# Conditional layer on quarters of TensorE, last contexts one product later, first block's weight sums one by one

## The chip, the cores and the metric

The kernel runs on one core of a Trainium2 chip. The metric is the device time of one execution in microseconds (us), the median of several runs. The profiler recorded one execution more; its times, and its "span" from the first to the last instruction, are what the views below show. The engines are TensorE (PE, with its weight loads as PEld), VectorE (DVE), ScalarE (ACT), GpSimd (POOL) and SyncE (SP), which here only issues DMAs. [...]

## What is computed

`x` is 64 batches of 64 rows with 1024 columns, 4096 tokens in all. Everything is float32, except where the last part quantises. Cut to what matters:

```python
def cond(x, condition, weights):            # weights: 16 x 64 x 64
    W = weights[condition]                  # one 64 x 64 matrix for each batch
    return einsum('bct,bcd->bdt', x, W)

def attn(x, qkvw, qkvb, ow, ob):            # 32 heads of 32
    q, k, v = split(x @ qkvw + qkvb)
    probs = softmax(q @ k.T / sqrt(32))     # within a batch of 64 rows
    return (probs @ v) @ ow + ob

x = x + attn(cond(x, itok, cond_weights), ...)
x = x + ffn(cond2(x, ...), ...)             # routed low-rank layer, quantised gated layer
```

Only the conditional layer, the attention and the first part of its output projection are touched by the change. The rest (`second_stage`) follows and stays as it is.

## The kernel before

**Tiling.** Two batches make a tile of 128 partitions (`x_t`), four tiles a block of 512 tokens (`PB = 4`), and there are `NBLK = 8` blocks. All large products (queries, keys, values, output) use a Winograd form of Strassen's scheme: a matrix of weights is cut in quarters A11 to A22 and a matrix of tokens in quarters B11 to B22, and seven products of quarters replace eight. Four sums of weight quarters (S1 to S4) and four of token quarters (T1 to T4) are needed. The products are issued in `Winograd.ORDER = (1, 6, 7, 5, 2, 4, 3)`; the weights are A11, S2, S3, S1, A12, A22, S4 and the tokens B11, T2, T3, T1, B21, T4, B22. Products 1 and 2 share a PSUM bank, as do 7 and 4, and 5 and 3: what was in the bank must have been read before the second one adds to it. In the profile the products appear by bank: `psqa`, `psqb`, `psqc`, `psqd`, then a, c and d again; `psk..` for keys, `psv..` for values, `po..` for the output. A query or key product is 8 matmul instructions in the trace, a value product 16: each matmul of float32 shows as two passes.

**The conditional layer.** `conditional(b, tiles)` makes B11 to B22 of a block. For each tile `j` of 128 tokens (two batches), the two 64x64 weights are gathered by POOL into `wg` and copied beside the diagonal's zeros into a 128x128 tile `wbd[j]` (L323, L375). A matmul (L350) then has 128 columns of `x` as the loaded operand and `wbd[j]` as the streaming one. Eight steps per block (`hf` for the half of the columns, `j` for the tile) have four matmuls each, in a bank of `ps_g`, which has four buffers. VectorE (L356, even `j`) or ScalarE (L358, odd `j`) copies the bank to `B`, and VectorE makes T1 to T4 (L366, L371) as soon as their quarters are there.

**The hand-written order.** `run(cost, product, rest)` issues PE's product, then the `rest` (copies, sums) of the product before (the list `behind`), and adds `cost` to a planned time `now`. Before each product it issues everything in `due` whose planned time has come. `phase(b, c, fills, length)` sets two groups of attention per phase (`group`, at the start and at half of the length): scores (L491, on quarters of TensorE, 64x64), the softmax on VectorE and ScalarE, a parting into halves of words (`ph`), a DMA transpose (`phT`), a joining (`pT`, ScalarE), and, in a later group, the context (L543). There are four phases per block. In the last one the `fills` between are the conditional layer, the first values job and the first query and key jobs of the block that follows. In the very last phase the fills are 14 products of the output projection, and the last contexts are set by `at(now + 41, contexts)`.

**Block 0.** The weights are loaded raw and S1 to S4 are made on the way: by VectorE for the first query job, by POOL for the first key and values jobs (`first_sums`), later by VectorE. `load_qk` and `load_v_raw` hand back a function that issues all four sums and the store; it is issued in one piece behind a product (`product_and_sums`, `with_sums`). In later blocks the sums are loaded from DRAM.

Of the kernel before, what the change touches and what calls it, by code (L numbers as in the profile page):

```python
# [182 lines left out]
def attention(tc, a, x_t, ctx_d, ident, dram, ps_g, KC, PB, NBLK, NCH, HPC, H, C, chores, early, op):  # L183
# [27 lines left out]
    with ExitStack() as ctx, ExitStack() as mid:  # L211
# [54 lines left out]

        RAW = ("A11", "A21", "A22", "A12")

        def sums(eng, at):
            eng.tensor_tensor(at("S1"), at("A21"), at("A22"), ALU.add)  # L270
            eng.tensor_tensor(at("S2"), at("S1"), at("A11"), ALU.subtract)
            eng.tensor_tensor(at("S3"), at("A11"), at("A21"), ALU.subtract)
            eng.tensor_tensor(at("S4"), at("A12"), at("S2"), ALU.subtract)

        w_qk, w_v = {}, {}
        later = []
# [1 line left out]
        def load_qk(b, wh, c, eng=None):  # L278
            t = w_qk[b, wh, c] = wp.tile([P, 7, KQ, P], F32, tag="wqk", name=f"w{wh}_{b}_{c}")
            if b == 0:  # L280
                if (wh, c) == ("q", 0):
                    held(t[:, SLOT["A11"], 0, 0:1], x_next[0][1])
                for key in RAW:
                    nc.sync.dma_start(t[:, SLOT[key], :, :], quarter(key, (0 if wh == "q" else H) + c * P, P))
                def rest():
                    sums(eng or nc.vector, lambda key: t[:, SLOT[key], :, :])
                    nc.gpsimd.dma_start(qk_d[wh, c], t)
                return rest
            nc.sync.dma_start(t, qk_d[wh, c])

        def load_v(b, g, slot):
# [3 lines left out]
        def load_v_raw(g, eng):  # L295
            for slot in range(7):
                w_v[0, g, slot] = w.tile([P, KQ, VC], F32, tag=f"wv{slot}", name=f"wv{slot}_0_{g}")

            def at(key):
                return w_v[0, g, SLOT[key]]  # L300

            for key in RAW:
                nc.sync.dma_start(at(key), quarter(key, 2 * H + g * VC, VC))

            def rest():
                sums(eng, at)
                for slot in range(7):
                    later.append(lambda slot=slot: nc.gpsimd.dma_start(v_d[g][:, slot, :, :], w_v[0, g, slot]))
            return rest

        bqkv = act.tile([P, 3 * KC], F32, tag="bqkv", name="bqkv")
        x_next = load_x(0)
        first_sums = [load_qk(0, "q", 0), load_qk(0, "k", 0, nc.gpsimd)]
        nc.sync.dma_start(bqkv, a["qkvb_t"])
        first_sums.append(load_v_raw(0, nc.gpsimd))

        wbd = []  # L320
        for j in range(PB):
            t = w.tile([P, P], F32, tag=f"wbd{j}", name=f"wbd{j}")
            nc.vector.memset(t, 0.0)  # L323
            wbd.append(t)
        kbd, vbd = [], []
        for u in range(4):
            t = act.tile([P, 2, HB], F32, tag=f"kbd{u}", name=f"kbd{u}")
# [8 lines left out]

        def conditional(b, tiles):

            def one(hf, j):
                key = f"B{hf + 1}{j // 2 + 1}"  # L340
                box = []

                def product():
                    xt = tiles[j][0]
                    if j % 2 == 0:
                        B[key] = yp.tile([P, KQ, HB], F32, tag=key, name=f"y{key}_{b}")
                    ps = ps_g.tile([P, 4, P], F32, tag="g", name=f"cond_{b}_{j}_{hf}")
                    for q in range(KQ):
                        k = hf * KQ + q
                        nc.tensor.matmul(ps[:, q, :], xt[:, k * P:(k + 1) * P], wbd[j], start=True, stop=True)  # L350
                    box.append(ps)

                def rest():
                    dst = B[key][:, :, (j % 2) * P:(j % 2 + 1) * P]
                    if j % 2 == 0:
                        nc.vector.tensor_copy(dst, box[0])  # L356
                    else:
                        nc.scalar.copy(dst, box[0])  # L358
                    if (hf, j) == (0, 3):
                        t_of("T1", "B12", "B11")  # L360
                    elif (hf, j) == (1, 3):
                        t_of("T2", "B22", "T1")
                        t_of("T3", "B22", "B12")
                    elif (hf, j) == (1, 1):
                        B["T4"] = B["B12"]
                        nc.vector.tensor_tensor(B["T4"], B["B21"], B["T2"], ALU.subtract)  # L366
                return 0.95, product, rest

            def t_of(key, x, y):
                B[key] = yp.tile([P, KQ, HB], F32, tag=key, name=f"{key}_{b}")  # L370
                nc.vector.tensor_tensor(B[key], B[x], B[y], ALU.subtract)  # L371

            for j, (_, wg) in enumerate(tiles):
                for r in range(2):
                    (nc.gpsimd if b else nc.vector).tensor_copy(wbd[j][halves[r], halves[r]], wg[halves[r], :])  # L375
            return [one(0, j) for j in range(PB)] + [one(1, j) for j in (2, 3, 0, 1)]

        def job(name, cost, n, matmuls, put, begin=None, done=None):


            banks, u = {}, {}

            def one(i):
                def product():
                    if i == ORDER[0] and begin:
                        begin()
                    bank = BANK[i]
                    first = bank not in banks
                    if first:
                        banks[bank] = ps_g.tile([P, 512], F32, tag="g", name=name.format(bank))  # L390
                    matmuls(i, banks[bank], first)
                    if done:
                        done(i)

                def rest():
                    ps = banks[BANK[i]][:, 0:n]
                    if i == 1:
                        u[1] = p1.tile([P, 512], F32, tag="p1", name=name.format("p1"))[:, 0:n]
                        nc.scalar.copy(u[1], ps)
                    elif i in (6, 7):  # L400
                        u[i] = p1.tile([P, 512], F32, tag=f"u{i}", name=name.format(f"u{i}"))[:, 0:n]
                        nc.vector.tensor_tensor(u[i], ps, u[1 if i == 6 else 6], ALU.add)
                    else:
                        m, t, v = {5: (1, 1, 7), 2: (0, 0, None), 4: (1, 0, 6), 3: (0, 1, 6)}[i]
                        put(m, t, ps, u.get(v))
                return cost, product, rest

            return [one(i) for i in ORDER]

        def biased(dst, ps, bias, u):  # L410
            if u is None:
# [1 line left out]
            else:  # L413
                nc.vector.scalar_tensor_tensor(dst, ps, bias, u, ALU.add, ALU.add)  # L414

        def rows_job(b, c, wh, next_load):

            qT = None

# [24 lines left out]
                if i == ORDER[-1] and next_load:  # L444
                    next_load()

            return job(f"ps{wh}{{}}_{b}_{c}", 1.72, HB, matmuls, put, begin, done)

        def values_job(b, g, next_load):

# [170 lines left out]
        def qk_fill(b, c):  # L621
            fills = []
            for wh in "qk":
                n = qk_jobs.index((b, wh, c))

                def next_load(n=n):
                    if n + 2 < len(qk_jobs):
                        f = load_qk(*qk_jobs[n + 2])
                        if f:
                            pending_sums.append(f)  # L630

                js = rows_job(b, c, wh, next_load)
                if b == 0 and n >= 2:

                    cost, product, rest = js[5]

                    def product_and_sums(product=product):
                        product()
                        if pending_sums:
                            pending_sums.pop(0)()  # L640
                    js[5] = (cost, product_and_sums, rest)
                fills += js
            return fills

        v_raw = []

        def v_fill(b, g):
            def next_load(slot):
                if b == 0 and g + 1 < NV:
                    if slot == SLOT[A_OF[ORDER[-1]]]:  # L650
                        v_raw.append(load_v_raw(g + 1, nc.vector))
                    return
                nxt = (b, g + 1) if g + 1 < NV else (b + 1, 0)
                if nxt[0] < NBLK:
                    load_v(*nxt, slot)
            js = values_job(b, g, next_load)
            if (b, g) == (0, 0):
                cost, product, rest = js[4]

                def product_and_sums():  # L660
                    product()
                    pending_sums.pop(0)()
                js[4] = (cost, product_and_sums, rest)
            return js

        for f in conditional(0, x_next):
# [7 lines left out]
        for b in range(NBLK):  # L674
            if b + 1 < NBLK:
                x_next = load_x(b + 1)
            for c in range(NP):
                fills, length = [], None
                if c + 1 < NP:
                    fills += qk_fill(b, c + 1)  # L680
                    if c == 0:
                        fills[7:7] = v_fill(b, 1)
                        if b == 0:
                            cost, product, rest = fills[4]

                            def with_sums(product=product):
                                product()
                                v_raw.pop()()
                            fills[4] = (cost, with_sums, rest)
                elif b + 1 < NBLK:  # L690

                    fills += conditional(b + 1, x_next) + v_fill(b + 1, 0) + qk_fill(b + 1, 0)
                else:
# [2 lines left out]
                    op.open_rest()  # L696
                    fills += op.pair(0) + op.pair(1)
                    length = 24
                    at(now + 41, contexts)
                if b + 1 == NBLK and c == 1:  # L700
                    assert next(chores, None) is None
                    early.close()
# [972 lines left out]
```

## Time and profile before

| | us |
|---|---|
| three runs | 2479.37, 2483.23, 2483.56 (median 2483.23) |
| the profiled execution | 2482.55 |
| its span, first to last instruction | 2480.8 |
| PE busy | 2435.7 (98% of the span) |
| DVE busy | 1524.9 (61%) |
| ACT busy | 953.6 (38%) |
| POOL busy | 360.8 (15%) |
| mean granted clock of TensorE | 0.992 of full |

The chain that ended last is "followed back from the last instruction: at each step to what released it, or to the instruction before it on its engine":

```profile
PE 95%; DVE 3%; DMA 1%; issue 1%; ACT 0%; SPq 0%; ACTq 0%; DVEq 0%
```

All waits of PE for another engine that last more than 3 us in total (us in total, times, longest):

```profile
PE cond L350 <- DVE wbd L375: 9.2, 1, 9.2
PE qTp_u L1427 <- DVE qb_u L1420: 7.2, 1, 7.2
PE c L543 <- ACT pT L533: 5.9, 1, 5.9
PE qTp_i L1427 <- DVE qb_i L1420: 3.9, 2, 2.8
PE cond L350 <- DVE yB L356: 3.2, 7, 0.5
```

The first is the start of the kernel, the second and fourth lie in its last 40 us, which the change doesn't touch. How to read a line of the views: in the chain, start, duration, engine, what, source line and number of merged instructions; in the utilisation of a stretch, its bounds and length, then the busy time of PE, PEld, DVE, ACT and POOL with the number of instructions, the granted clock, the busy share of the DMA engines and GB/s. "issue" is time in which an engine waited for nothing that the profile shows.

### The profile page before, as it was taken

What the parts mean: (1) busy time and instruction counts of PE and PEld (TensorE: products, weight loads), DVE (VectorE), ACT (ScalarE), POOL (GpSimd) and SP (SyncE); (2) the same over time, 40 slices, a digit from 0 to 9 for tenths busy, and PEclk for the clock granted to TensorE, in tenths of its full rate; (3) what the DMA queues carried; (4) which work ended last, traced back from release to release, by engine and by line L of the source; (5) the groups of instructions that cost most, each with busy time, mean ns of one, the idle gap of its engine ahead of it and who ended that gap; (6) DMA issues with size and microseconds to landing.
All of it is one profiled execution on the core that took longest, in us unless ns stands there. A gap on an engine that the chain in (4) does not pass through costs nothing.

```text
span 2480.8 us, 34182 instructions
## 1 busy us (share of the span) xinstructions
PE 2435.7 (98%) x13232; PEld 1703.8 (69%) x13232; DVE 1524.9 (61%) x2957; ACT 953.6 (38%) x1303; POOL 360.8 (15%) x451
## 2 busy tenths in 40 slices
PE   8999999999999999999999999999999999999996
PEld 7888888888888888888888644444454545454452
DVE  4585585675764755745646623333367777778787
ACT  1243353443443533533534533343423333333333
POOL 5010011011122221110000233334200000000001
PEclk9999999999999999999999999999999999999997
DMA  8795767676677667766646668877744443434343
GB/s 281 262 266 153 225 192 232 191 208 203 205 201 246 206 188 248 201 202 181 171 145 215 187 213 248 271 232 239 227 151 79 87 79 81 85 73 91 71 96 70
DMA packets 417980, 446.76 MB, mean 180 GB/s; under 512 B 299665, under 2 KB 353938, under 8 KB 404114
## 3 DMA queue, kind: packets, MB, share of 16 engines
q1 hardware_dynamic: 387298, 377.90, 52.5%
q0 software_dynamic: 12080, 49.82, 7.6%
q10 hardware_dynamic: 18432, 16.79, 2.0%
q8 instruction: 106, 1.74, 0.3%
q14 instruction: 64, 0.52, 0.1%
HBM read 272.97 MB, written 100.66 MB: 151 GB/s over the span
## 4 chain that ended last, share of the span: by engine, by line
PE 95%; DVE 3%; DMA 1%; issue 1%; ACT 0%; SPq 0%; ACTq 0%; DVEq 0%
PE pska L428 5%; PE psva L455 5%; PE poc L1019 5%; PE pskc L428 4%; PE psvc L455 4%; PE pskd L428 4%; PE psqd L428 4%; PE pbc L1019 4%; PE pba L1019 4%; PE psvd L455 4%; PE psqa L428 4%; PE poa L1019 4%; PE pod L1019 4%; PE pbd L1019 4%; PE psqc L428 4%; PE s L491 3%
## 5 line engine op out<-in xcount | busy, mean ns | idle before, releaser
L533 ACT COPY pT<-phT 128x1024 int16<-128x1024 int16 x128 | 167.2, 1342 | 84.8 <-DMA phT<-ph 84.6
L553 ACT ACTIVATE co<-c,bqkv 128x256 f32<-128x256 f32 x128 | 60.6, 473 | 295.2 <-PE c L543 253.6
L503 DVE TENSOR_REDUCE mx<-s 128x8 f32<-128x512 f32 x128 | 88.3, 690 | 138.0 <-PE s L491 128.4
L521 ACT COPY ph<-prob 128x1024 int16<-128x1024 int16 x128 | 131.4, 1046 | 43.4 <-DVE prob L515 42.7
L414 DVE SCALAR_TENSOR_TENSOR kbd<-pskd,bqkv,psku 32x256 f32<-32x256 f32 x256 | 122.6, 479 | 30.9 <-PE pskd L428 27.2
L507 ACT ACTIVATE prob<-prob 128x512 f32<-128x512 f32 x128 | 78.9, 628 | 154.4 <-DVE prob L504 130.6
L1140 POOL TENSOR_TENSOR xo<-xo,ob 128x1024 f32<-128x1024 f32 x32 | 82.5, 2597 | 375.7 <-DMA xo<-in_x_dram 371.2
L428 PE MATMUL psqa<-yB,wq 128*128 128x256 f32 x512 | 123.5, 384 | 0.0
L428 PE MATMUL pska<-yB,wk 128*128 128x256 f32 x512 | 122.6, 382 | 0.0
L1483 POOL DMA_DIRECT2D out_dram<-y x29 | 25.2, 869 | 653.4 <-DVE y L1475 653.4
L1114 ACT COPY xh<-xo 128x1024 int16<-128x1024 int16 x64 | 64.1, 1040 | 143.8 <-DVE xo L1159 143.4
L455 PE MATMUL psva<-wv,yB 128*128 128x256 f32 x512 | 117.7, 383 | 0.0
L1019 PE MATMUL poa<-woA,cx 128*128 128x512 f32 x256 | 115.3, 593 | 0.0
L1019 PE MATMUL pba<-wtA,x1T 128*128 128x512 f32 x256 | 115.1, 592 | 0.0
L1125 ACT COPY xTo<-xhT 128x1024 int16<-128x1024 int16 x64 | 84.8, 1341 | 64.1 <-DMA xhT<-xh 62.3
L455 PEld LDWEIGHTS psva<-wv,yB 128*128 128x128 f32 x512 | 96.8, 191 | 13.4
L428 PEld LDWEIGHTS pska<-yB,wk 128*128 128x128 f32 x512 | 96.0, 190 | 14.3 <-issue 1.4
L428 PEld LDWEIGHTS psqa<-yB,wq 128*128 128x128 f32 x512 | 95.2, 190 | 13.7 <-issue 0.2
L513 DVE TENSOR_REDUCE den<-prob 128x8 f32<-128x512 f32 x128 | 86.8, 678 | 17.4 <-ACT prob L507 17.2
L504 DVE TENSOR_TENSOR prob<-s,mx 128x512 f32<-128x512 f32 x128 | 88.6, 692 | 9.7 <-DVE mx L503 0.9
L515 DVE TENSOR_TENSOR prob<-prob,den 128x512 f32<-128x512 f32 x128 | 89.8, 702 | 4.4
L412 ACT ACTIVATE kbd<-pska,bqkv 32x256 f32<-32x256 f32 x128 | 59.6, 466 | 79.2 <-PE pska L428 77.6
(243 smaller groups left out, 5138.5 us busy)
## 6 DMA issues: line engine op xcount, KB each, us to landing
wv<-v_d SPq DMA_DIRECT2D x98, 512.0 KB, 3.8
wq<-q_d SPq DMA_DIRECT2D x28, 1792.0 KB, 8.1
wk<-k_d SPq DMA_DIRECT2D x28, 1792.0 KB, 8.2
x<-in_x_dram SPq DMA_DIRECT2D x32, 512.0 KB, 9.8
ctx_d<-co ACTq DMA_DIRECT2D x128, 128.0 KB, 5.6
cx<-ctx_d SPq DMA_DIRECT2D x16, 1024.0 KB, 7.0
xo<-in_x_dram SPq DMA_DIRECT2D x32, 512.0 KB, 5.7
xT_d<-xTo SPq DMA_DIRECT2D x64, 256.0 KB, 4.1
```

The source lines that it names most:

```text
L414: nc.vector.scalar_tensor_tensor(dst, ps, bias, u, ALU.add, ALU.add)
L428: nc.tensor.matmul(ps[:, 0:HB], A[:, SLOT[A_OF[i]], k, :], B[B_OF[i]][:, k, :], start=first and k == 0, stop=k == KQ - 1, skip_group_check ...
L455: nc.tensor.matmul(ps[:, j * VC:(j + 1) * VC], B[B_OF[i]][:, k, j * P:(j + 1) * P], A[:, k, :], start=first and j == 0 and k == 0, stop=k ...
L503: nc.vector.tensor_reduce(mx_v, ps, AX.X, ALU.max)
L504: nc.vector.tensor_tensor(p.rearrange("p (a e) k -> p a e k", a=2), ps, mx_v.unsqueeze(3).to_broadcast([P, 2, HPC, C]), ALU.subtract)
L513: nc.vector.tensor_reduce(den, p, AX.X, ALU.add)
L515: nc.vector.tensor_tensor(p, p, den.unsqueeze(2).to_broadcast([P, n, C]), ALU.mult)
L521: nc.scalar.copy(h, planes(p.rearrange("p n k -> p (n k)")))
L533: nc.scalar.copy(planes(pT.rearrange("p a b q -> p (a b q)")), hT)
L1019: self.nc.tensor.matmul(ps, self.B[self.B_OF[i]][:, k, :], self.A[self.A_OF[i]][:, k, :], start=first and k == 0, stop=k == self.KQ - 1, s ...
L1125: nc.scalar.copy(planes(xT.rearrange("p k q -> p (k q)")), hT)
L1140: nc.gpsimd.tensor_add(s["x"][:, t, :], s["x"][:, t, :], self.ob)
```

## The change

Four things are changed.

1. The conditional layer works on 64x64 quarters of TensorE. There is no `wbd`; the gathered `wg` streams directly. Each of four steps per block makes a whole tile `j`, with two banks (one for each half of the rows, that is for each batch) and 32 matmuls of 64x64x64. VectorE empties the first bank and ScalarE the second, each in two copies of 256 columns. T1 to T4 all come after the last tile. The planned costs are four times 1.2 in place of eight times 0.95.
2. Sums of weights are a list of four instructions instead of one function. They are issued one or two at a time ahead of products (`with_sums`): the `wv` sums one each ahead of fills 3 to 6, the query and key sums two each ahead of products 5 and 6 of a job.
3. The very first query job takes its products in the order (1, 2, 6, 7, 5, 4, 3). As 1 and 2 share a bank, the rest of 1 is issued ahead of 2.
4. The last contexts are planned at 44.5 instead of 41, which is one product of the output projection later.

```diff
-        def sums(eng, at):
-            eng.tensor_tensor(at("S1"), at("A21"), at("A22"), ALU.add)
...
+        def sums(eng, at, stored):
+            def last():
+                eng.tensor_tensor(at("S4"), at("A12"), at("S2"), ALU.subtract)
+                stored()
+            return [
+                lambda: eng.tensor_tensor(at("S1"), at("A21"), at("A22"), ALU.add),
+                lambda: eng.tensor_tensor(at("S2"), at("S1"), at("A11"), ALU.subtract),
+                lambda: eng.tensor_tensor(at("S3"), at("A11"), at("A21"), ALU.subtract),
+                last,
+            ]
...
-            def one(hf, j):
+            def one(j):
+                banks = []
                 def product():
-                    for q in range(KQ):
-                        k = hf * KQ + q
-                        nc.tensor.matmul(ps[:, q, :], xt[:, k * P:(k + 1) * P], wbd[j], start=True, stop=True)
+                    xt, wg = tiles[j]
+                    for r in range(2):
+                        banks.append(ps_g.tile([P, KC, C], F32, tag="g", name=f"cond{r}_{b}_{j}"))
+                    for k in range(KC):
+                        for r, f in ((0, 0), (1, 1), (0, 1), (1, 0)):
+                            nc.tensor.matmul(
+                                banks[r][halves[f], k, :], xt[halves[r], k * P + f * C:k * P + (f + 1) * C],
+                                wg[halves[r], :], start=True, stop=True,
+                            )
                 def rest():
+                    for hf in range(2):
+                        key = f"B{hf + 1}{j // 2 + 1}"
+                        if j % 2 == 0:
+                            B[key] = yp.tile([P, KQ, HB], F32, tag=key, name=f"y{key}_{b}")
+                        for r in range(2):
+                            t0 = (j % 2) * P + r * C
+                            src = banks[r][:, hf * KQ:(hf + 1) * KQ, :]
+                            if r == 0:
+                                nc.vector.tensor_copy(B[key][:, :, t0:t0 + C], src)
+                            else:
+                                nc.scalar.copy(B[key][:, :, t0:t0 + C], src)
+                    if j == PB - 1:
                         t_of("T1", "B12", "B11")
                         t_of("T2", "B22", "T1")
                         t_of("T3", "B22", "B12")
                         B["T4"] = B["B12"]
                         nc.vector.tensor_tensor(B["T4"], B["B21"], B["T2"], ALU.subtract)
-                return 0.95, product, rest
+                return 1.2, product, rest
-            return [one(0, j) for j in range(PB)] + [one(1, j) for j in (2, 3, 0, 1)]
+            return [one(j) for j in range(PB)]
...
+                    if order[1] == i == 2:
+                        behind.pop()()
...
-                js = rows_job(b, c, wh, next_load)
+                js = rows_job(b, c, wh, next_load, (1, 2, 6, 7, 5, 4, 3) if n == 0 else ORDER)
                 if b == 0 and n >= 2:
-                    js[5] = (cost, product_and_sums, rest)
+                    for at_, count in ((5, 2), (6, 2)):
+                        with_sums(js, at_, pending_sums, count)
...
+        def with_sums(fills, i, sums, count):
+            cost, product, rest = fills[i]
+            def product_and_sums():
+                for _ in range(min(count, len(sums))):
+                    sums.pop(0)()
+                product()
+            fills[i] = (cost, product_and_sums, rest)
...
                         if b == 0:
-                            fills[4] = (cost, with_sums, rest)
+                            for at_ in range(3, 7):
+                                with_sums(fills, at_, v_raw, 1)
...
-                    at(now + 41, contexts)
+                    at(now + 44.5, contexts)
```

## The prediction

> **What bounds the kernel now.** I read the page first: PE is busy 98% of 2480.8 us and has 95% of the chain of waits. A change can only pay where that chain leaves PE, or where it makes PE's own stream shorter. So I then read the chain in order of time around the three places that the diff touches, and single instructions on the timeline. First a block boundary (0 to 1; the other six have the same starts to 0.1 us):
>
> ```profile
> 181.62 1.08 PE s L491 x32
> 182.72 0.70 DVE mx L503
> 183.52 0.69 DVE prob L504
> 184.21 0.38 DVE kbd L414
> 186.11 0.69 DVE yB L356
> 186.80 0.61 DVE mx L503
> 187.50 0.69 DVE prob L504
> 188.19 0.61 DVE yB L356
> 188.85 2.94 PE cond L350 x24
> 191.79 3.49 PE psva L455 x16
> ```
>
> Between the scores `s` and the first values product `psva` the chain runs through VectorE. The utilisation of that stretch says the same: VectorE is busy 12.86 of 14 us, against 94.73 of 157 in the rest of the block.
>
> ```profile
> 182.00:196.00 14.00, 13.55 (x141) 12.60 (x134) 12.86 (x21) 9.02 (x13) 0.00 (x0) 1.00 0.43 151
> 196.00:353.00 157.00, 157.00 (x1105) 136.31 (x1107) 94.73 (x184) 61.76 (x93) 9.99 (x22) 1.00 0.66 198
> ```
>
> Second, block 0: four sums of `wv` stand together on VectorE, and PE's seventh query product waits behind them; the last line is the utilisation from 82 to 90 us, where the 0.79 is the granted clock.
>
> ```profile
> 77.61 1.14 DVE wv L270
> 79.92 1.23 DVE wv L272
> 82.31 0.49 DVE qT L414
> 82.85 2.88 PE psqd L428 x8
> 85.73 4.25 PE psva L455 x16
> ...
> 82.00:90.00 8.00, 7.15 (x25) 5.99 (x26) 4.18 (x8) 0.00 (x0) 3.70 (x7) 0.79 0.56 173
> ```
>
> Third, the last block: PE runs dry inside the last contexts, until a transpose lands, and the next product takes 5.31 us instead of 3.43 because the clock was halved.
>
> ```profile
> 1429.13 7.30 DMA phT<-ph
> 1436.45 1.35 ACT pT L533
> 1437.84 1.12 PE c L543 x16
> 1438.97 5.31 PE poc L1019 x8
> 1444.27 3.43 PE pod L1019 x8
> ```
>
> [...] 32 passes of the scores on quarters take 1.03 us in the chain, so one set of four 128-column passes takes some 0.11 us [...], what one full-array 128-column pass takes too. [...] a stall of 3.0 us at 79.8 and one of 5.9 us at 1431.9 are followed by half clock, while 1.6 us at 19.7 is not.
>
> **The change part by part.** Durations are of the profiled execution, which took 2482.55 us (span 2480.8); that is 0.7 below the median 2483.23, so I sum on 2482.55.
>
> *Conditional products.* Now 64 passes of 128 columns per block, 24 in 2.94 us near the end (others 0.112 us each): 64 x 0.112 = 7.2 us. After: 256 quarter passes in 64 sets of four, 64 columns wide. The trace has no such form; the nearest is the context (64 columns, two side by side): 64 passes in 2.02 us, the second 32 in 0.94, so 0.058 us a set. 64 x 0.058 = 3.7 us if four side by side are no slower than two, 7.4 us if each pass needs its 0.029 us of issue. I take 3.7: scores already have four side by side at one set's price. [...] So PE's stream is 3.5 us shorter per block, 0.2 longer at the other end.
>
> What is late next: VectorE. At a boundary its order in the new emission is: `mx`, `prob`; `kbd` x4; copies of tile 0; `mx`, `prob`; copies of tile 1; the normalisation; copies of tiles 2 and 3; T1; T2. Spacings from the timeline: mx to prob 0.79, prob 0.61, kbd 1.99 in all, the three normalisation steps 1.56, T1 1.28 to a T2 that needs it, T2 1.22. A 128x512 copy takes 0.69 (0.61 apart); a 128x256 PSUM operation (`psqu`) 0.42, 0.34 apart. Eight of the latter stand before T2 (2.72) in place of three of the former (1.83): +0.89. One normalisation of the two that stood before T2 now comes after: -1.56. From 182.72: 1.40 + 1.99 + 0.68 + 1.40 + 0.68 + 1.56 + 1.36 + 1.28 + 1.22 = 11.57, so T2 ends at 194.3, against 194.8 seen. `psvb`, which needs T2, started at 195.12, when `psva` ended, and can start at 194.35 if `psva` starts by 190.8. It does if it gets a bank that ScalarE empties (190.0); with one that VectorE empties (191.2) `psvb` starts at 194.85. Gain 0.3 to 0.77; I take 0.6, so 4.2 for seven boundaries. ScalarE's eight 256-column copies replace four of 512, and one `pT` copy (1.36) comes before tile 3's; they end by 191.9, before T1 needs them only just. The planner's phase is 2.8 shorter, so the double contexts move from before the last values product to just ahead of a query job. There the fifth product after them needs ScalarE's exponents and the sums behind these: it would wait 0.6, 1.1 and 0.1 us in blocks 2, 3 and 7 with the DMA waits seen there, and something like the 1.1 us that the present order loses at 564 goes. I take 1.2 off. Sum of boundaries: 3.0.
>
> The eight `wbd` copies a block (POOL, 0.23 us each) and VectorE's eight in block 0 go; their cover was full, except for 0.5 us at 8.7, where PE can start at once on the gathered weight. The next block's gathers now wait on POOL until the products have read `wg`, some 20 us later than at 170; behind them are only weight chores, which have a block's time.
>
> *Opening of block 0.* [...] Tile 3's weight lands at 12.35, and its product ends near 14.2. VectorE then makes the `wq` sums (their second operand lands at 14.57: 14.6 to 17.3), tile 3's copies, T1, T2 (20.5). PE meanwhile does product 1 (14.35 to 16.1), waits 0.5 for ScalarE's copy of the bank, does product 2 (to 18.4) and waits for T2; product 6 starts at 20.5 (now 21.34) with two products behind it instead of one: 5 x 1.73 later keys start at 29.2 instead of 31.8. Gain 2.6. [...]
>
> *Sums spread.* Now VectorE reaches `qT` of product 5 at 82.31. In the new order it stands after two `wv` sums instead of four: 79.8. The fifth product waits for `psqu` behind the first sum (78.75) and the seventh for that `qT` (80.3): so `psva` starts at 82.3 and `psvb` at 85.8 instead of 89.8. The idle time is 1.0 us[...]. Gain 4.0 (both counted without the 2.6). The other key and query sums only move by one product.
>
> *Last contexts.* The product of 3.43 us is put into the stall: PE would reach the contexts at 1433.6, do three quarters of them by 1435.3 and wait 2.55 us instead of 5.94 for the same transpose, whose queue isn't touched. That gives 3.4 us; and 1.9 more where no clock window is halved, which 2.55 us may or may not do. I take 4.3.
>
> Sum: 3.0 + 2.6 + 4.0 + 4.3 = 13.9, so 2468.65 on the profiled execution and 2469 for a median.
>
> **Rivals.**
> (1) *PE's saving reaches the path.* If VectorE had slack at the boundary, 3.3 us would come seven times: 23 in place of 3, so 2448. For it: the planner books 4.8 for 7.6. Against: the chain above, with VectorE full until T2.
> (2) *Quarters bound by issue.* At 7.4 us of products per block boundaries give nothing or lose 0.2 each, the opening gives 2.1, the contexts 3.4: gain 2.1 + 4.0 + 3.4 - 1.4 = 8.1, so 2474.5; to 2479 if the spread sums or the contexts meet a new wait of their own. For it: `c` shows gaps called issue at 1072 to 1074.
> (3) [...] PE now waits in three or four pieces there, some 3.5 us within 7, where it waited 0.5. [...] Against: a window that is 52% busy (18.9 to 22.4) kept the full clock, and I count 54% in the worst one.
> (4) *The stall only moves*: the sums do no good, 2473; inside the range.
>
> **How the numbers follow.** Forecast 0.64; (1) 0.06; (2) with (4) 0.18; (3) 0.12. Under 0.2% (5 us) a measurement of this kernel can't tell from no change. The forecast case is faster wholly; of (2) 0.12 faster and 0.06 same; of (3) 0.02 same, 0.10 slower. So faster 0.82, same 0.08, slower 0.10. The forecast's own range is 2463 to 2475. Below, boundaries at 0.8 to 1.0 and no halved clock at the end give 2461; above, (2) reaches 2479. The range 2461 to 2480 leaves out (1) and most of (3).
>
> **What would show it.** In the new trace: sets of four quarter passes 0.055 to 0.06 us apart (0.115 would be rival 2); `psvb` 13.1 to 13.3 us after the start of `s` at each boundary (13.5 now), with PE idle some 4 us between and VectorE without a gap from `mx` to T2; keys of block 0 starting near 29; no half clock near 77 to 85; contexts at the end waiting near 2.5 us after one more product. The prediction is wrong if `psva` starts 3 us earlier at boundaries (rival 1), or runs at half clock there (rival 3).

## The result and the profile after

| | before, us | after, us |
|---|---|---|
| median (range) of 9 runs each | 2483.23 (2478.49 to 2487.47) | 2490.95 (2486.36 to 2495.20) |
| profiled execution | 2482.55 | 2494.39 |
| its span | 2480.8 | 2492.5 |
| PE busy | 2435.7 | 2422.1 |

The ratio is 1.0034, 95% interval 1.0022 to 1.0046: 0.34% slower, where 0.6% faster was forecast. TensorE has 13.6 us less to do and the kernel takes longer, so new idle time must stand on its path. The chain of waits by engine of the changed kernel shows which kind has grown:

```profile
PE 94%; DVE 3%; issue 1%; DMA 1%; ACT 1%; SPq 0%; ACTq 0%; DVEq 0%
```

To the whole percent "issue" is 1% before and after, but now it stands ahead of DMA. It is time in which an engine waits for nothing that the profile shows, so the profile names no semaphore and no other engine for it. The list of TensorE's waits (total, times, longest) in the changed kernel says where it has grown; the single line below is the only one for issue in the same list of the kernel before:

```profile
PE cond L348 <- issue: 20.1, 10, 4.3
...
PE cond L348 <- DVE kbd L417: 9.1, 7, 1.3
```

```profile
PE c L543 <- issue: 1.8, 3, 1.0
```

The line on issue is the new one: ten pieces, up to 4.3 us, in front of the quarter products. The timeline of TensorE shows two boundaries of the changed kernel (start, length, what, number of matmul records, in brackets the idle time ahead and its cause); the first two lines are the boundary into block 2, the last three that into block 6:

```profile
356.49 1.03 PE L348 MATMUL cond<-wg,x 64*64 64x64 f32 x52 [1.30 <-DVE kbd L417]
359.71 3.44 PE L348 MATMUL cond<-wg,x 64*64 64x64 f32 x125 [2.19 <-issue]
...
1055.76 1.97 PE L348 MATMUL cond<-wg,x 64*64 64x64 f32 x117 [1.30 <-DVE kbd L417]
1062.07 2.37 PE L348 MATMUL cond<-wg,x 64*64 64x64 f32 x73 [4.33 <-issue]
1064.37 4.43 PE L458 MATMUL psva<-wv,yB 128*128 128x256 f32 x16
```

The gap lies in the middle of a product, between two matmuls that need nothing new. At five of the seven boundaries it is followed by half clock: here the granted clock is 0.50 from 1062.43 to 1065.84, and `psva` takes 4.43 us instead of 3.6. The seven boundaries don't lose equally; from the start of the scores `s` to that of `psvb` they take 14.32, 16.06, 17.00, 16.34, 17.97, 17.55 and 13.53 us, each of them 13.57 before.

What comes in during a gap is seen in the DMA queues of a narrow stretch, 357.0 to 358.6 us (packets, MB, share):

```profile
q8 instruction: 1, 0.02, 3.7%
```

One packet on the queue that carries instructions, in flight from 357.44 to 358.39; TensorE goes on at 359.71. The same line of the whole page, before and after:

```profile
q8 instruction: 106, 1.74, 0.3%
```

```profile
q8 instruction: 118, 1.93, 0.3%
```

Twelve more such fetches. The page of the changed kernel counts 14,768 matmuls and as many weight loads, 1,536 more of each than before (13,232): 3,072 / 12 = 256 instructions per fetch. The single packets have 16,384 bytes, so 64 bytes for an instruction.

The places of the gaps fit blocks of 256 as well. The longest gap for issue comes after 220 of the 256 passes on quarters in block 0, and after 163, 118, 195, 148, 228, 183 and 136 at the seven boundaries. Counted round a block, which is 128 passes with their 128 weight loads, that is 57 passes earlier at the first boundary and 45 to 51 earlier from each to the next. From the start of one conditional layer to that of the next TensorE has 2674 instructions in the trace, and then 2909 to 2912, which is 114 and 93 to 96 more than whole blocks of 256: 57 and some 47 passes. So where TensorE stops, a block of instructions ends, whatever the product is doing there.

The difference of the two profiled executions, 11.7 us, by place: opening of block 0 +2.1 (first key product at 33.89, was 31.80), spread sums -4.0, boundaries up to `psvb` +17.8, the rest of the blocks -1.1, after the last boundary to TensorE's end -4.1 (of it the last contexts -2.2), behind that +1.1.

### The profile page after: what moved, and what is told of

Read it like the earlier page. It is cut to its first block, busy times and chain, and to the rows that moved or that the text cites. A ratio compares the mean times of both kernels' runs of the same rounds, so it can differ in the third digit from the quotient of the medians.

```text
span 2492.5 us, 37285 instructions
## 1 busy us (share of the span) xinstructions
PE 2422.1 (97%) x14768; PEld 1688.3 (68%) x14768; DVE 1526.9 (61%) x2977; ACT 956.9 (38%) x1335; POOL 348.3 (14%) x395
## 4 chain that ended last, share of the span: by engine, by line
PE 94%; DVE 3%; issue 1%; DMA 1%; ACT 1%; SPq 0%; ACTq 0%; DVEq 0%
PE psva L458 5%; PE pska L431 5%; PE psvd L458 4%; PE pskc L431 4%; PE psvc L458 4%; PE pskd L431 4%; PE pbc L1015 4%; PE pba L1015 4%; PE psqc L431 4%; PE pod L1015 4%; PE psqd L431 4%; PE poa L1015 4%; PE poc L1015 4%; PE pbd L1015 4%; PE psqa L431 4%; PE s L494 3%
## 5 line engine op out<-in xcount | busy, mean ns | idle before, releaser
L1015 PEld LDWEIGHTS poa<-woA,cx 128*128 128x128 f32 x256 | 48.5, 190 | 60.4 <-issue 60.0
```

What stands on the lines that cost most here:

```text
L1015: self.nc.tensor.matmul(ps, self.B[self.B_OF[i]][:, k, :], self.A[self.A_OF[i]][:, k, :], start=first and k == 0, stop=k == self.KQ - 1, s ...
```

## The experiments

Two theories stood against each other for the boundaries. **S, supply:** TensorE's instructions come in blocks of 256, and a stage of 512 in 4 us empties what is at hand faster than fetches refill it. **D, disturbance:** the quarters stall for another reason (the array's mode, waits for data, other DMAs in the way). The kernel before ran beside each group again: 2478.48 us (the four runs x), 2483.24 (y), 2481.57 (z).

### The parts taken apart: x1 and x4

x1 is the changed kernel with the conditional layer of before:

```
-            def one(j):            # quarters, two banks
+            def one(hf, j):        # full array with wbd, one bank
```

> The changed kernel with the conditional layer as it was before (full array, zeros beside the diagonal, eight steps); the other three parts of the change stay. Supply theory (PE runs out of instructions in the quarter products): the boundaries lose nothing, the spread sums keep their 4 us and the later contexts some 2 to 4, so 2475 to 2480 us, with no idle PE called issue inside the conditional products. Rival, the loss sits in the order of the sums, the opening or the contexts: 2487 or more.

x4 is the kernel before with the quarters alone.

> The kernel before with the quarters alone: sums, first order and contexts as before. Supply theory: the boundaries lose the 16.6 us that the two traces differ by there, and nothing is won elsewhere: 2494 to 2502 us. Rival, the parts of the change disturb each other (the other order of the sums makes the boundary late): 2480 to 2488.

| | median, us | ratio to before (95%) |
|---|---|---|
| x1_full_array | 2470.75 | 0.9968 (0.9956 to 0.9981) |
| x4_only_quarters | 2504.81 | 1.0104 (1.0084 to 1.0124) |

x1 is shorter and x4 longer than forecast. So the quarters do the harm, and the rest of the change is worth 7.7 us. x4 loses 26.3 us: by its trace 19.1 at the boundaries, and 3.9 in the opening, where TensorE waits 4.5 us for T2. In x1 no wait for issue stands in front of a conditional product; its boundary is that of before, 13.57 us seven times (timeline of TensorE, boundary into block 6):

```profile
1041.77 2.94 PE L354 MATMUL cond<-wbd,x 128*128 128x128 f32 x24 [0.45 <-DVE yB L360]
1044.55 3.66 PE L461 MATMUL psva<-wv,yB 128*128 128x256 f32 x16
```

In x4 they are all back, in a kernel that shares nothing else with the change:

```profile
PE cond L344 <- issue: 19.4, 10, 3.6
```

### Half the instructions: x2

```
-                        for r, f in ((0, 0), (1, 1), (0, 1), (1, 0)):
-                            nc.tensor.matmul(banks[r][halves[f], k, :], xt[halves[r], k * P + f * C:k * P + (f + 1) * C], ...)
+                        for r in range(2):
+                            nc.tensor.matmul(banks[r][:, k, :], xt[halves[r], k * P:(k + 1) * P], ...)
```

> The changed kernel with the conditional products on two halves of the rows (64 rows, all 128 columns of the loaded operand) instead of four quarters: 128 passes per block instead of 256, same banks, same copies, same array time if the two halves run side by side. Supply theory: half the instructions, so the idle PE called issue inside the conditional products falls from 20 us to under 4 and the time to 2468 to 2478 us. Rival, the emptying of the banks by VectorE and ScalarE or the switch of the mode makes the loss: nothing changes, 2488 to 2494. Rival, the loads of 128 columns don't run side by side: 7.2 us of products, 2476 to 2482.

Measured: 2479.98 us, ratio 1.0006 (0.9997 to 1.0014). Two row halves of the array instead of four quarters, 256 instructions a stage: no wait for issue of 0.2 us or more, boundaries of 13.70 us. That speaks for S. But the halves brought no speed, as this boundary shows (64*128 is the tile of the array):

```profile
357.07 2.22 PE L348 MATMUL cond<-wg,x 64*128 64x64 f32 x34
359.63 5.54 PE L348 MATMUL cond<-wg,x 64*128 64x64 f32 x94 [0.34 <-DVE kbd L417]
```

94 passes in 5.54 us are 0.059 us each, one after the other; had the two halves run side by side, it would be half. The time is that of the second rival. So x2 slows the demand as well and can't separate the count from the pace. It also lost 5.7 us in the opening (first key at 37.57): VectorE could begin a tile's copies only every 3.41 us there (12.59, 16.00, 19.41), 0.107 us a pass instead of 0.059.

### Another transfer in the way: x3

The 1.8 MB load of key weights that starts at each boundary is put off by 14 us of the schedule's time.

```
+                        if c == NP - 1 and wh == "k":
+                            at(now + 14, lambda: load_qk(*qk_jobs[n + 2]))
```

> The changed kernel with the one load of 1.8 MB of key weights that starts with each boundary put off by 14 us of planned time, into the values job. Supply theory with contention (the fetch of instructions comes late because its packets stand behind these of the weights): the first and longest gap at each boundary shrinks from 2 to 4 us to under 1.5, and the time falls to 2479 to 2486 us. Supply theory without contention (a fetch takes its 3.6 us whatever else runs): the gaps stay, 2488 to 2493.

Measured: 2488.13 us, ratio 1.0039 (1.0024 to 1.0053), the same as the changed kernel. The waits come after the same number of passes (118, 195, 148, 228 and 182 where they are longest), and are a quarter less in sum; with the load in its place three traces have 20.1, 20.9 (y4) and 19.4 us (x4). In x3:

```profile
PE cond L348 <- issue: 15.6, 8, 4.2
```

That load is not the main cause; whether it has a part in it can't be told from one trace, and the time shows none. But the run shows what a boundary is without starvation: two of the seven (the first is below) had no wait for issue of over 0.7 us, and took 12.77 us.

```profile
185.41 1.95 PE L348 MATMUL cond<-wg,x 64*64 64x64 f32 x93 [0.66 <-issue]
187.29 3.72 PE L458 MATMUL psva<-wv,yB 128*128 128x256 f32 x16
190.97 3.72 PE L458 MATMUL psvb<-wv,T 128*128 128x256 f32 x16
```

`psvb` starts 0.05 us after VectorE has ended T2 (190.92). So the bound that the prediction computed, VectorE up to T2, is real, and appears when the supply lets it.

### The same quarters in another order: y1, y2, y3

```
-                    fills += conditional(b + 1, x_next) + v_fill(b + 1, 0) + qk_fill(b + 1, 0)
+                    fills += cf[0:2] + vf[0:2] + cf[2:4] + qf[0:2] + vf[2:] + qf[2:]
```

Here `cf`, `vf` and `qf` are the conditional, value and query/key products, with values and first query job in the order 1,2,6,7,5,4,3. Not an instruction of a product is added or left out; only 7 us of full-array products come between the second and third tile, in which a fetch can land. y2 has the full array in block 0 in addition, y3 is y2 with the first scores of a boundary behind the first two tiles.

> The changed kernel with the same quarters, the same instruction count per conditional product, at seven boundaries in another order: products of tiles 0 and 1, value products 1 and 2, products of tiles 2 and 3, query products 1 and 2, then the rest of values and query (the value and query job of a boundary run in the order 1,2,6,7,5,4,3). Theory S (the supply of TensorE's instructions bounds the stage, 256 instructions of each 512 are at hand when it begins): no conditional product waits for issue at the boundaries, so the issue waits in front of the conditional's line fall from 20.1 us to under 2.5 (the opening's 1.14 stays), no half clock behind them, and the seven boundaries save about 3.5 us each against the full array of x1_full_array (the full-array stage takes 7.2 to 7.8 us, the quarters 3.7): 2470.75 - 7 x 3.5 + 2.1 for the opening, about 2448, range 2442 to 2458. Rival Q (a quarter pass itself is slow, or the quarters wait for their data): the waits stay, 15 to 20 us in sum, wherever the products are put, and the time stays at 2482 to 2492. Rival V (VectorE is the bound at the boundary): the waits for issue go, but waits of value product 6 for T2 take their place, 3 us at each boundary, and the time is 2465 to 2475.

> As y1_spread_quarters, but block 0 alone has its conditional layer on the full array as before. Theory S and the reading of the opening (quarters cost 2.1 us there, the full array nothing): first key product begins at 31.8 instead of 33.9, time 2 us under y1_spread_quarters, about 2446. Rival (the opening costs the same either way because later waits absorb it): within 0.5 us of y1_spread_quarters.

> As y2_spread_full_opening, and at the seven boundaries the scores of the first group come behind the conditional products of tiles 0 and 1 instead of ahead of them. Theory: the wait of TensorE for kbd at the start of the boundary (9.1 us in 10 waits in the changed kernel) and the wait of value product 1 for its inputs are covered by each other's work: 1 to 1.5 us a boundary, 7 to 10 us in all, about 2437. Rival: the softmax of the group runs 2.4 us later and its contexts wait that much longer at the middle of the phase: 2446 to 2450.

| | median, us | ratio to before (95%) |
|---|---|---|
| y1_spread_quarters | 2502.82 | 1.0080 (1.0064 to 1.0096) |
| y2_spread_full_opening | 2507.26 | 1.0096 (1.0082 to 1.0110) |
| y3_spread_late_scores | 2517.66 | 1.0143 (1.0128 to 1.0157) |

The times missed by some 55 to 80 us. As to the cause the runs say more. TensorE's waits in y1:

```profile
PE psqc L431 <- DVE psqu L405: 12.0, 8, 2.0
...
PE cond L348 <- issue: 6.8, 4, 2.5
PE psva L458 <- ACT psvp L402: 4.7, 7, 0.7
...
PE psqa L431 <- ACT psqp L402: 3.7, 8, 0.5
...
PE cond L348 <- ACT vbd L471: 2.8, 7, 0.4
```

The waits for issue fall from 20.1 to 6.8 us, where under 2.5 were forecast; 2.1 of these are the opening's. Five of seven boundaries have none over 0.5 us, the two others have theirs after 238 and 216 matmuls and weight loads. In y3, where scores and contexts follow the first two tiles in the same breath, the quarters themselves wait 0.3 us for issue in all, and the wait turns up in the contexts instead, which have no part in the change (boundary into block 6):

```profile
1066.78 1.04 PE L592 MATMUL c<-pT,vbd 128*64 128x64 f32 x28
1071.43 0.47 PE L592 MATMUL c<-pT,vbd 128*64 128x64 f32 x4 [3.62 <-issue]
```

So it falls on whatever comes when the instructions at hand are used up; D, which ties it to the quarters, can't explain that. The time was lost to my order. Product 2 directly behind product 1 waits for ScalarE's copy of their common bank (`psvp`, `psqp`), the third tile for the bank of value product 2 (`vbd`), and in the query job 7,5,4 puts one product between the two that share bank c instead of two: product 4 then waits for a sum that stands behind softmax on VectorE, 12.0 us in eight waits. y2's full array in block 0 won nothing (first key at 31.76, 31.94 in y1; the intervals of the two overlap). y3 showed in addition that the 9.1 us of `kbd` are not the scores' wait: it stayed at 8.7, since the second tile waits for the bank that the last key product leaves.

### Fewer quarters: z1

Tiles 0 and 2 on quarters, tiles 1 and 3 and all of block 0 on the full array: 320 instructions in a stage.

```
-            return [one(j) for j in range(PB)]
+            return [one(0), whole(1), one(2), whole(3)]
```

> As x1_full_array (block 0 on the full array), but at the seven boundaries tiles 0 and 2 of the conditional layer on quarters, tiles 1 and 3 on the full array: 320 TensorE instructions in the stage instead of 512 (quarters) or 128 (full array), spread over about 5.7 us (2 x 1.08 and 2 x 1.8). Theory S (instruction supply, 256 and a rest at hand): no wait for issue of 1 us or more in front of the conditional's lines at the boundaries, no half clock behind them; VectorE's chain to T2 is then the bound, scores to value product 6 in 12.8 us instead of 13.57: 7 x 0.77 = 5.4 us under x1_full_array, about 2465 (2463 to 2469). Rival (any quarters disturb, for instance by the switch between forms of matmul): waits of 1 to 4 us stay at some boundaries, boundaries 14 us or more, time 2474 or more.

Measured: 2467.53 us, ratio 0.9944 (0.9930 to 0.9957). A boundary (into block 6) on TensorE, then the line on issue at the boundaries' full-array products:

```profile
1035.71 1.16 PE L394 MATMUL cond<-wg,x 64*64 64x64 f32 x64
1036.81 1.16 PE L433 MATMUL cond<-wbd,x 128*128 128x128 f32 x8
1038.27 1.13 PE L433 MATMUL cond<-wbd,x 128*128 128x128 f32 x8 [0.31 <-DVE kbd L489]
1039.33 1.16 PE L394 MATMUL cond<-wg,x 64*64 64x64 f32 x64
1041.01 2.02 PE L433 MATMUL cond<-wbd,x 128*128 128x128 f32 x16 [0.51 <-issue]
1042.87 3.62 PE L530 MATMUL psva<-wv,yB 128*128 128x256 f32 x16
1046.44 3.72 PE L530 MATMUL psvb<-wv,T 128*128 128x256 f32 x16
```

```profile
PE cond L433 <- issue: 2.8, 6, 0.5
```

In front of the quarters themselves there is one such wait, at the boundary into block 4, which takes 13.47 us:

```profile
698.91 0.57 PE L394 MATMUL cond<-wg,x 64*64 64x64 f32 x22 [0.98 <-issue]
```

A tile on quarters takes 1.1 us here (start to start), on the full array 1.86 (the last). `psvb` begins 12.84 us after `s` (1033.60) and 0.05 after T2's end (1046.39). The seven boundaries take 12.84 to 13.47 us, mean 13.01, and `psva` 3.62 behind this one. So quarters as such don't disturb. Going over between quarters and the full array four times in a stage costs at most the gap of 0.51 us that stands before the last tile. S holds.

### The opening: y4 and z4

VectorE's T2 and T3 and a sum of GpSimd in the changed kernel (timelines of the two engines):

```profile
21.22 2.10 DVE L375 TENSOR_TENSOR T<-yB,T 128x1024 f32<-128x1024 f32 x1
23.24 2.28 DVE L375 TENSOR_TENSOR T<-yB,yB 128x1024 f32<-128x1024 f32 x1
```

```profile
22.31 2.13 POOL L276 TENSOR_TENSOR wk<-wk 128x512 f32<-128x512 f32 x1
```

Elsewhere they take 1.22 and 1.27. y4 is the changed kernel with GpSimd's sums held back until T4 is there.

```
+        gate = sm.tile([P, 1], F32, tag="gate", name="gate")
+        nc.gpsimd.tensor_copy(gate, B["T4"][:, 0, 0:1])
         for f in first_sums[4:]:
```

> The changed kernel, where GpSimd begins its sums of the first key weights only when VectorE has finished T4 of block 0 (about 3 us later). Theory P (VectorE's T2, T3, T4 are slow at the opening because GpSimd sums beside them): T2 to T4 take 1.22 us each instead of 2.10, 2.28, 2.17, the sums 1.27 each instead of 1.67 to 2.24, query product 6 starts 0.9 us sooner (22.5 instead of 23.37), the first key product 0.9 to 1.7 us sooner (32.2 to 33.0 instead of 33.89), the time 1 to 2 us shorter, 2489. Rival (the T's are slow for another reason, their buffers or the DMA into SBUF): they stay at 2.1 to 2.3, key products wait for their weights, time unchanged or longer.

```profile
20.52 1.23 DVE L375 TENSOR_TENSOR T<-yB,T 128x1024 f32<-128x1024 f32 x1
21.66 1.22 DVE L375 TENSOR_TENSOR T<-yB,yB 128x1024 f32<-128x1024 f32 x1
```

As theory P said, to the hundredth. The first key product starts at 30.54 (33.89 in the changed kernel), sooner than forecast: of the 3.35 us T2 makes 0.9; 1.8 come from a stretch of half clock (granted clock 0.50 from 24.78 to 28.19 in the changed kernel, where products 6 and 7 take 2.30 and 3.04 us start to start; in y4 1.83 and 1.73); and 0.7 from the query sums, which begin at 15.81 instead of 16.52 because their load landed sooner, in which the edit has no part. Side by side both engines stretch, VectorE's sums from 1.22 to 2.10 and 2.28 us and GpSimd's from 1.27 to 2.13; neither takes the 2.49 us of one after the other. But the time stayed, 2491.86 us, ratio 1.0036 (1.0023 to 1.0048): in this execution the starved boundaries took 2.7 us more than in the changed kernel's. A few us can't be told in runs whose supply starves now here, now there.

z4 is x1 with the first query job in the plain order.

> As x1_full_array, with the first query job in the plain order 1,6,7,5,2,4,3. Theory (the order 1,2,6,7,5,4,3 brings nothing where the conditional layer is on the full array, because the first key product began at 31.84 against 31.80 before): first key product at 31.8 within 0.3, time within 0.5 us of x1_full_array. Rival (the order hides what the 1.2 us later sums of the query weights cost): first key product about 1.5 us later, 33.3, time 1.5 us over x1_full_array.

Measured: 2472.35 us, ratio 0.9966 (0.9952 to 0.9979), x1's within the interval. The first key starts at 33.16, as the rival said: from the first query product on it takes 13.98 us, in x1 12.82 (19.02 to 31.84). The order does hide 1.16 us; x1 looked like no gain because its conditional layer happened to end 1.2 us later than before's.

### The last contexts: z2 and z3

z2 is the kernel before with 44.5 for 41 alone.

> The kernel before with the last contexts at 44.5 instead of 41 and nothing else. Theory: the contexts' wait for pT falls from 5.94 by the 3.43 us of one output product, to about 2.5, and all of it reaches the end: 3.4 to 3.7 us shorter, ratio 0.9986. Rival (given back in the tail, as 0.8 to 2 us were in the changed kernel): 1.5 to 2.2 us shorter, ratio 0.9992.

Measured: 2476.56 us, ratio 0.9982 (0.9972 to 0.9991), so 2 to 7 us shorter. The wait for `pT` falls from 5.94 to 3.4, and from the last `psvb` of a boundary to TensorE's end it takes 1244.4 us instead of 1247.4: 3.0 shorter.

z3 is z1 with the second scores of the last phase one product sooner (`length = 20` for 24).

> As z1_two_tiles_quarters, and in the last attention phase the second group of scores begins one output product sooner (at 10 instead of 12 of the model's time). Theory: its pT is ready 3.4 us sooner, so that the 2.65 us of TensorE that the last contexts still wait for pT in x1_full_array go: 2.6 us under z1_two_tiles_quarters, 2462. Rival: the second scores wait for the first group's softmax to free their bank, or the chain to pT is bound by the transposing DMAs: within 0.5 us of z1_two_tiles_quarters or slower.

Measured: 2463.61 us, ratio 0.9926 (0.9913 to 0.9940), the shortest median of all: 18.0 us under the kernel before beside it (its interval overlaps z1's). The contexts run in one piece:

```profile
1428.18 2.08 PE L618 MATMUL c<-pT,vbd 128*64 128x64 f32 x64
```

In its profiled execution three boundaries of the seven still starved, into blocks 2, 4 and 7 (14.15, 13.54 and 15.62 us), in z1's one. The wait of the last; the 14 passes behind it take 0.22 us each, where the 16 of z1 take 0.126:

```profile
1214.54 3.09 PE L433 MATMUL cond<-wbd,x 128*128 128x128 f32 x14 [1.10 <-issue]
```

So 320 instructions are near the edge, not safely below it.

## Why the prediction was wrong

**The step that failed** is the price of the quarters: "64 x 0.058 = 3.7 us if four side by side are no slower than two, 7.4 us if each pass needs its 0.029 us of issue. I take 3.7". A pass was taken as bounded by the array or by the engine's own issue; that the instructions have to be brought in was not counted. As long as they are at hand the quarters are almost that fast: 1.1 us a tile, 4.4 for four. An estimate from the block fetches that follow each other in a starved stretch (708.09, 711.99 and 715.27 in the changed kernel): 256 instructions take 3.3 to 3.9 us to come (on average 3.6, the figure in x3's expectation), 13 to 15 ns each, and a tile of 128 wants them at 8.6. By the same counts, an estimate too, at most one block and a rest is at hand at the start: the longest gaps come 236 to 457 matmuls and weight loads into a stage. Then TensorE waits for the block: at 708 the wait begins 1.0 us before the fetch, which takes 0.96, and ends 1.2 us after it has landed, 3.2 us in all.

```profile
710.28 2.81 PE L348 MATMUL cond<-wg,x 64*64 64x64 f32 x108 [3.19 <-issue]
```


Rival 2 ("bound by issue") was nearest in kind, but too mild. Its 7.4 us spreads a slow issue evenly, and boundaries then lose at most 0.2. In fact the shortage comes in one or two lumps, most of them in the stage's second half, and at five of seven boundaries half clock follows them (granted clock 0.50 for 3.41 us from 359.28, 536.78, 710.86 and 1062.43, and for 6.8 us from 884.94; 1.00 at every boundary before). Against 12.77 us without starvation the mean boundary takes 16.11: 7 x 3.34 = 23.4, of which some 19 are the waits for issue (20.1 less the opening's 1.14) and most of the rest a slower `psva`, 29.8 us in all where seven without starvation would take 25.9 (3.7 each). Rival 3 (slower, 2483 to 2495 us, by half clock at the boundaries) foresaw that loss and its sign, with another cause: it let PE wait for VectorE in several small pieces. When half clock would come, and the price it put on it, were the author's estimates.

What the prediction had in hand: it quoted gaps "called issue" in the contexts at 1072 to 1074 of the kernel before, where small matmuls stand close too, and did not ask what they were. A fetch was in flight there (1071.80 to 1072.67); whether it is the same shortage was not tested.

**Boundaries, VectorE as the bound.** Right where it could show: 12.77 to 12.85 us without starvation, against 12.8 from its sum at best ("194.35" less 181.55). The 0.77 us at its upper end was the truer value than the 0.6 taken. The seven come to 5.0 to 5.6 us, of which z1 collects 3.9 (7 x 0.56). Two small terms of the prediction have their numbers in the kernel before: the sets of four passes of the scores start 0.109 us apart (181.71 to 182.36), and the 0.2 us longer in PE's stream, an estimate for one more change of the array's form, compares with 0.14: the first 32 passes of the contexts behind the scores take 1.08 us, the next 32 0.94 (213.51 to 215.53).

**New waits in mid-block** ("I take 1.2 off" the gain): they did not come; the rest of the blocks is 1.1 us shorter.

**Opening.** Key products were forecast at 29.2 and came at 33.89, 4.7 later. Three terms failed. The second operand of the query sums was put at 14.57; VectorE waited for its load until 16.52, and T2 began 1.9 us late. T2 was priced at 1.22 and took 2.10, since GpSimd's sums, which follow the query sums, ran beside it: 0.9. And full clock behind the waits was an estimate that failed: from 24.78 to 28.19 the granted clock was 0.50, products 6 and 7 took 2.44 and 3.21 us, and the five products 1.9 longer.

```profile
16.52 0.69 DVE L275 TENSOR_TENSOR wq<-wq 128x512 f32<-128x512 f32 x1 [1.12 <-DMA wq<-in_qkvw_dram]
23.37 2.44 PE L431 MATMUL psqb<-T,wq 128*128 128x256 f32 x8 [1.97 <-DVE T L375]
25.67 3.21 PE L431 MATMUL psqc<-T,wq 128*128 128x256 f32 x8
```

The last tile's quarters starved here as well (1.14 us), but VectorE was still at the query sums when they were done, so that cost nothing. x3 and y1 have the same opening; their keys began at 32.15 and 31.94. The order 1,2,... alone is worth 1.16.

**Spread sums.** Exact: "`psvb` at 85.8 instead of 89.8" before the opening's shift. In the changed kernel:

```profile
80.89 1.99 PE L431 MATMUL psqc<-yB,wq 128*128 128x256 f32 x8 [0.70 <-DVE psqu L405]
...
87.90 3.62 PE L458 MATMUL psvb<-wv,T 128*128 128x256 f32 x16
```

85.8 + 2.1 for the late opening is 87.9. One wait of 0.70 is left of 3.0, and the granted clock is 1.00 from 75 to 92 us (before it was 0.50 from 83.80 to 87.21).

**Last contexts.** The mechanism was right, 4.3 was too much. The wait was put at 2.55 us; it was 4.16, 2.65 (x1) and 3.4 (z2), and in all three the product behind still takes 5.4 us instead of 3.6 (granted clock 0.50 from 1454.96 to 1458.38 in the changed kernel, from 1435.48 to 1442.30 before).

```profile
1454.22 0.69 PE L546 MATMUL c<-pT,vbd 128*64 128x64 f32 x16 [4.16 <-ACT pT L536]
1454.83 5.40 PE L1015 MATMUL pod<-woS,cx 128*128 128x512 f32 x8
```

So up to the product behind 2.2 us in the changed kernel, 3.0 alone, 3.7 in x1. The term "1.9 more where no clock window is halved" (5.31 less 3.43 in the kernel before) was to be had: in z1 the wait was 2.12 us and the product behind took 3.70.

```profile
1429.06 0.69 PE L618 MATMUL c<-pT,vbd 128*64 128x64 f32 x16 [2.12 <-ACT pT L608]
1429.67 3.70 PE L1087 MATMUL pod<-woS,cx 128*128 128x512 f32 x8
```

By the sum: 4.0 came as forecast, 4.3 came as 2.2 (3.0 up to the last instruction), 2.6 as -2.1, 3.0 as -16.6 (17.8 lost, 1.1 won).

## What to carry to other kernels

Splitting a matmul over parts of the array multiplies its instructions (512 for 128 in a stage here): count those of a stage, not only its passes, and compare their number with what is at hand (at most one block of 256 and a rest here) and their pace with the 13 to 15 ns each estimated here. An "issue" wait between two matmuls that need nothing new, with a 16 KB packet on the instruction queue beside it, was the sign here; fewer instructions (z1: 3.8 us of such waits instead of 20.1) or slower work between them (y1: 6.8) relieved it, and splitting only as far as the next bound reaches (two tiles of four here) was worth more than splitting all (2467.53 us against 2490.95). When an engine's work is moved, ask what it will run beside: VectorE's T2 and T3 took 2.10 and 2.28 us beside GpSimd's sums, 1.22 without them (y4).

## What was not expected of the hardware

- A starved TensorE waits up to 4.33 us at a time (changed kernel), where a whole tile's products on the full array take 1.86 (z1); in the changed kernel the five boundaries whose longest wait was 2.19 to 4.33 us had a granted clock of 0.50 for 3.41 or 6.8 us, and the two with 1.76 and 1.58 us kept 1.00.
- Two row halves of the array (64x128) with 64 moving columns in float32 showed no overlap: 0.059 us a pass (x2), where four quarters take 0.017 us a pass (z1: 64 in 1.10 us).
- The same boundaries starve more in one profiled execution and less in another (into block 1 14.32 us in the changed kernel and 15.79 in y4, into block 5 17.97 and 14.91), though the gaps lie at the same passes; what decides how late a fetch is was not found. x3 excludes only that one load as the main cause.
